# Two stands of four tiled matmul batches per group instead of three stands, in a kernel whose order is a table

## The chip, the cores and the metric

The kernel runs on one core of one Trainium2 chip. The metric is the device time of one execution in microseconds (us), as the median of several runs. Five instruction streams work side by side and meet at semaphores: TensorE (PE in the profile, its weight loads are PEld), VectorE (DVE), ScalarE (ACT), GpSimd (POOL) and SyncE (SP), which issues DMAs here.

## The reference: what is computed

The input x is 128 batches of 128 tokens by 512 features, in float32; adj is a 128 x 128 matrix. Two layers follow each other.

```python
# layer 0: with W1 = W2 = adj, (C - A) is the bias b alone
A = jnp.einsum('od,bdn->bon', adj, x)
pre = A[:, :, None, :] + (C - A)[:, :, :, None]
x = layernorm(x + jnp.max(relu(pre), axis=-1))
# layer 1: 8 heads of 64 features, mask from adj
qkv = x @ w_qkv
attn = softmax(where(adj == 0, -inf, q k^T * 64**-0.5))
o = (attn @ v) @ w_proj + b_proj
x = layernorm(x + o + layernorm(o) * gamma + beta)
```

Because both weights of layer 0 are adj, its branch comes to one number per token: the maximum over the features of adj times x, plus b, clipped at zero.

## The kernel before

Batches are worked in 32 groups of four. Every step of one batch (or of one of a group's twelve dense products) is a small Python function; the table `STEADY` gives each step a place in time relative to its group, `PERIOD` is the distance of two groups, and `group_plan` puts all steps of all groups on one list, which is sorted by place. The steps are then issued in that order, each to its engine. So the places only decide the order in which each engine's queue is filled; at run time an engine takes its queue strictly in that order, and waits where an input or a buffer isn't ready. The first two groups have tables of their own (`FIRST`), and so do the last two (`LAST`); `SETUP` places the weights' preparation. `TWO` says which of the alternating steps go to GpSimd, or into a pair of PSUM banks. `HOMES` names the buffer of each tile, by batch in the group and by group.

The steps, by engine, for batch i of a group (0 to 3; a number behind a step's name is i, or the dense product's number 0 to 11):

- SP: `load` (x, 256 KB), `xrow` and `xcross` (the normalized x is written to DRAM as 16-bit planes and read back by a transposing DMA), `row` and `cross` (the same for the attention weights, 512 KB), `res` (x again, for the residual), `out`.
- PE: `conv` (adj times x, 2 matmuls of 512 columns as float32 needs two passes), `dm` and `dd` (a dense product of q, k or v in three terms: eight matmuls of high and low parts, four of the difference form), `S` (scores, 8 heads), `AV` (attention times v, 8 heads), `po` and `pod` (the output projection, eight and four matmuls).
- DVE: `bn`, `ba`, `cmax` (maximum of conv), `xmask`, `xsub` (high and low part of x), `rest` (adds the difference product), `masked`, `rmax`, `recip`, `wts` (softmax), `omask`, `osub`, `pmain`, `prest`, `n1a`, `n1b`.
- ACT: `norm0`, `xpl`, `main` (evicts the eight-matmul product), `exps`, `pln`, `sq0`, `sq1`, `sq2`, `norm2`, `add0`, and high halves `xhigh`, `ohigh`.
- POOL: `relu`, statistics of a column each (`rstdx`, `shiftx`, `rstd0`, `shift0`, `sm1`, `st1`, `sm2`, `st2`), `resx`, `resb`, `reso` (the residual), and those differences `xd`, `od` and high halves that `TWO` gives it.

The scores use 64 rows of the array (a head has 64 features), and attention times v 64 columns; all other matmuls use 128 by 128. In the steady order S and AV stand next to each other in runs between the other matmuls, called stands here. The products' matmuls are float32r, those of `conv`, `S` and `AV` float32.

Each step's lines are in the functions below: `load` L626, `conv` L630, `S` L863, `AV` L949, the products L817, L818 and L823, `bn` L680, `prest` and `n1b` L1012. Some buffers are few: x tiles (`xt` and `xT`) have four slots, which loads and transposed copies share; the eight PSUM banks are four single ones (`ps1`) and two pairs (`ps2`); `planes` and `xplanes` have one buffer each.

Of the kernel before, what the change touches and what calls it, by code (L numbers as in the profile page):

```python
# [27 lines left out]
PERIOD = 55.65721  # L28
STEADY = {
    'load': [-84.387, -101.525, -92.757, -104.895],  # L30
    'conv': [-75.113, -75.979, -71.238, -73.133],
    'cmax': [-74.046, -74.912, -70.171, -71.594],
    'relu': [-73.282, None, -69.407],
    'bn': [-79.685, -90.339],
    'ba': [-78.963, -87.311],
    'rstdx': [-71.500],
    'shiftx': [-67.749],
    'add0': [None, None, -69.067, -62.343],
    'sq0': [None, None, -68.228, -60.929],
    'rstd0': [None, None, -60.228],  # L40
    'shift0': [None, None, -20.160],
    'norm0': [-66.552, -60.223, -55.338, -56.756],
    'xpl': [-65.714, -57.708, -54.441, -46.941],
    'xrow': [-64.641, -56.635, -53.368, -45.398],
    'xcross': [-61.931, -52.928, -48.082, -41.718],
    'xmask': [-54.951, -43.405, -41.164, -36.407],
    'xsub': [-48.801, -42.437, -37.819, -35.400],
    'xhigh': [-46.997, -35.315, -37.063, -35.835],
    'xd': [-26.327, -29.608, -22.523, -17.793],
    'dm': [4.837, 11.201, 6.655, 16.122, -27.595, -10.169, -22.140, -32.141, -33.960, -23.959, -25.777, -30.323],  # L50
    'dd': [9.383, 10.292, 20.788, 27.152, -12.896, -6.532, -8.350, -5.623, -4.714, -16.490, -7.441, -11.987],
    'main': [7.711, 13.218, 9.668, 20.862, -11.380, -7.877, -11.865, -20.987, -31.942, -21.472, -23.760, -26.046],
    'rest': [10.516, 14.823, 28.292, 38.461, -10.247, -5.049, -3.873, -4.461, -2.608, -11.977, -6.331, -9.059],
    'S': [0.000, 0.997, 13.110, 14.107],
    'masked': [1.644, 5.106, 15.417, 27.161],
    'rmax': [3.380, 8.064, 24.101, 29.327],
    'exps': [4.623, 15.506, 26.003, 35.155],
    'recip': [10.406, 20.865, 29.217, 43.570],
    'wts': [11.110, 22.861, 30.453, 44.268],
    'pln': [13.703, 24.200, 32.382, 51.803],  # L60
    'row': [20.837, 26.467, 34.304, 55.119],
    'cross': [24.197, 29.995, 47.113, 59.806],
    'AV': [37.158, 54.685, 53.762, 70.756],
    'omask': [41.739, 55.758, 58.432, 77.236],
    'osub': [42.962, 56.693, 64.847, 80.884],
    'ohigh': [46.552, 56.528, 63.853, 84.748],
    'od': [47.794, 58.991, 74.103, 86.254],
    'po': [51.853, 58.675, 73.718, 96.599],
    'pod': [57.646, 64.130, 75.536, 100.236],
    'pmain': [60.163, 63.121, 81.492, 101.655],  # L70
    'prest': [61.894, 65.455, 82.210, 102.843],
    'res': [41.103, 53.159, 76.024, 78.628],
    'resx': [52.598, 58.118, 78.904, 82.973],
    'resb': [53.844, 60.258, 80.456, 101.811],
    'reso': [62.664, 71.516, 83.739, 104.286],
    'sq1': [66.881, 66.175, 85.753, 103.922],
    'sm1': [66.639, 71.226, 88.501, 103.613],
    'st1': [68.723, 67.062, 90.348, 105.534],
    'n1a': [69.485, 72.830, 94.712, 105.600],
    'n1b': [77.841, 75.237, 95.973, 108.029],  # L80
    'sq2': [78.635, 93.900, 96.767, 110.927],
    'sm2': [90.058, 96.472, 97.864, 110.751],
    'st2': [94.366, 98.154, 99.952, 125.624],
    'norm2': [95.548, 105.334, 102.729, 130.428],
    'out': [97.230, 106.460, 109.286, 132.611],
# [3 lines left out]
        'load': [-311.682, -309.097, -309.092, -289.177],  # L89
        'conv': [-301.956, -285.978, -284.699, -252.846],  # L90
        'cmax': [-276.686, -268.417, -252.229, -243.444],
        'relu': [-275.480, -258.624, -245.414, -236.373],
        'bn': [-298.400, -272.353, -260.336, -251.012],
        'ba': [-276.256, -271.589, -254.792, -248.969],
        'rstdx': [-272.599, -269.091, -248.273, -238.464],
        'shiftx': [-269.130, -253.340, -240.209, -232.976],
        'norm0': [-266.978, -249.667, -237.355, -228.662],
        'tx': [-266.046, -245.978, -230.203, -224.006],
        'copy': [-248.555, -225.163],
        'pv': [-226.671, -221.380],  # L100
        'keep': [-210.841, -209.446],
        'xmask': [-237.451, -231.282, -228.825, -220.542],
        'xsub': [-232.807, -226.381, -226.376, -184.540],
        'xhigh': [-235.047, -224.785, -216.680, -210.529],
        'xd': [-232.210, -205.597, -206.130, -125.910],
        'dm': [None, None, 8.596, 7.614, -27.333, -7.643, -16.082, -37.145, -46.738, -6.339, -11.225, -36.934],
        'dd': [None, None, 7.519, 13.277, -25.364, -7.365, -10.388, -25.470, -13.330, -4.235, -16.812, -26.914],
        'main': [None, None, 9.424, 14.292, -8.119, -5.070, -13.376, -26.832, -30.312, -2.548, -8.551, -26.673],
        'rest': [None, None, 11.233, 35.409, -6.802, -0.906, -5.599, -18.911, -0.865, 0.048, -7.653, -11.149],
        'S': [0.071, 3.526, 11.673, 10.965],  # L110
        'masked': [4.362, 7.230, 17.266, 20.450],
        'rmax': [4.711, 7.375, 18.562, 27.402],
        'exps': [6.391, 14.172, 25.847, 36.857],
        'recip': [12.522, 19.013, 30.495, 40.437],
        'wts': [13.400, 26.323, 35.020, 43.252],
        'pln': [14.511, 33.217, 37.332, 48.065],
        'row': [24.078, 40.304, 45.297, 48.373],
        'cross': [31.686, 41.648, 45.892, 58.796],
        'AV': [38.517, 48.815, 50.261, 70.407],
        'omask': [43.804, 51.125, 58.512, 81.275],  # L120
        'osub': [44.138, 53.164, 60.683, 86.080],
        'ohigh': [45.476, 55.853, 65.956, 87.153],
        'od': [52.512, 60.084, 71.048, 87.521],
        'po': [48.135, 56.775, 71.054, 93.215],
        'pod': [54.003, 61.222, 76.700, 97.775],
        'pmain': [55.811, 59.410, 82.388, 98.578],
        'prest': [56.183, 64.180, 82.945, 101.590],
        'res': [46.370, 42.491, 71.387, 79.013],
        'resx': [63.966, 47.589, 79.420, 100.786],
        'resb': [70.459, 70.785, 81.534, 105.046],  # L130
        'reso': [70.474, 72.568, 90.218, 105.110],
        'sq1': [63.146, 65.537, 87.020, 104.749],
        'sm1': [69.929, 71.912, 90.063, 105.360],
        'st1': [72.212, 72.233, 94.751, 105.573],
        'n1a': [78.126, 76.071, 96.130, 106.436],
        'n1b': [82.298, 76.869, 96.351, 108.235],
        'sq2': [82.739, 79.519, 97.605, 111.944],
        'sm2': [87.842, 82.457, 97.845, 117.109],
        'st2': [90.386, 87.300, 99.888, 120.030],
        'norm2': [95.187, 93.693, 107.047, 122.559],  # L140
        'out': [99.205, 96.285, 112.844, 132.585],
    },
    {
        'load': [-131.325, -146.629, -109.252, -117.493],
        'conv': [-103.575, -126.260, -90.173, -103.104],
        'cmax': [-94.745, -125.823, -83.341, -89.398],
        'relu': [-80.440, None, -75.846],
        'bn': [-106.480, -139.224],
        'ba': [-99.960, -134.812],
        'rstdx': [-91.047],  # L150
        'shiftx': [-79.188],
        'add0': [None, None, -74.243, -74.248],
        'sq0': [None, None, -69.318, -69.504],
        'rstd0': [None, None, -68.606],
        'shift0': [None, None, 14.252],
        'norm0': [-78.560, -74.678, -62.455, -54.484],
        'xpl': [-77.724, -72.376, -61.942, -52.495],
        'xrow': [-75.147, -66.114, -52.002, -51.491],
        'xcross': [-52.007, -55.219, -51.696, -50.648],
        'xmask': [-51.097, -51.522, -47.743, -46.741],  # L160
        'xsub': [-47.766, -48.031, -45.293, -45.741],
        'xhigh': [-44.210, -49.814, -42.689, -41.925],
# [31 lines left out]
        'n1b': [80.034, 71.944, 89.870, 107.555],  # L194
        'sq2': [83.515, 87.175, 100.626, 112.358],
        'sm2': [85.095, 77.407, 91.265, 112.382],
        'st2': [89.764, 89.887, 102.645, 129.724],
        'norm2': [94.880, 93.286, 102.685, 130.269],
        'out': [99.098, 100.886, 102.826, 130.308],
    },  # L200
# [951 lines left out]
```

## Time and profile before

| | us |
|---|---|
| median of three runs (1845.74 to 1847.9) | 1845.97 |
| the profiled execution | 1842.58 |
| its span | 1840.6 |
| TensorE busy in it | 1804.2 |
| VectorE, ScalarE, GpSimd busy | 1548.9, 1541.5, 1311.4 |
| mean granted TensorE clock | 0.996 |

The span goes from the first to the last instruction. A matmul's row has the time of its start and a modelled duration that overlaps the next one's, so distances of starts are what tells TensorE's pace. A wait is put down to what released it. "x330" behind an engine's busy time is the number of its instructions in the stretch. One line of the DMA view gives how long after its issue a transfer of a tile had landed. A stretch's line has, after the five engines, the granted clock, the DMA engines' share and GB/s.

### The profile page before, as it was taken

The numbers are of one execution on the slowest core, as the hardware profiler recorded it, in microseconds if no ns is written. First come the engines' busy times: TensorE is split into PE (matmuls) and PEld (weight loads), VectorE is DVE, ScalarE is ACT, GpSimd is POOL, SyncE is SP. The second block draws the span as 40 slices with busy tenths as digits, with TensorE's granted clock in tenths as the row PEclk, the third lists the DMA queues.
The fourth block names the chain that finished last, engine by engine and source line by source line (L and its number), as shares of the span: only waits on it lengthen the run. The fifth ranks groups of instructions, "written<-read, shape, count | busy, mean of one in ns | idle before, by whom it ended". The sixth has DMA issues, their size and how long they took to land. (4 is left out here: it accounts for less than half of the span.)

```text
span 1840.6 us, 32730 instructions
## 1 busy us (share of the span) xinstructions
PE 1804.2 (98%) x10541; PEld 1426.1 (77%) x10541; DVE 1548.9 (84%) x2584; ACT 1541.5 (84%) x3927; POOL 1311.4 (71%) x1935
## 2 busy tenths in 40 slices
PE   8999999999999999999999999999999999999995
PEld 5777777778777788777787777787777787777874
DVE  7988888888888888888888888888888888788877
ACT  6988888888888888888888888888888888878865
POOL 4277787677777777777676877776877777667768
PEclk9999999999999999999999999999999999999998
DMA  5556665666575676565676656675656665656641
GB/s 150 173 149 182 170 171 162 163 179 183 150 185 165 158 191 171 157 175 160 175 183 166 170 169 162 174 184 161 180 162 159 185 184 149 178 144 178 155 126 46
DMA packets 486139, 302.91 MB, mean 165 GB/s; under 512 B 399440, under 2 KB 403664, under 8 KB 485968
## 3 DMA queue, kind: packets, MB, share of 16 engines
q1 hardware_dynamic: 485104, 299.70, 60.6%
q8 instruction: 84, 1.38, 0.3%
q10 hardware_dynamic: 864, 1.12, 0.2%
q14 instruction: 87, 0.71, 0.1%
HBM read 72.16 MB, written 131.07 MB: 110 GB/s over the span
## 5 line engine op out<-in xcount | busy, mean ns | idle before, releaser
L902 ACT ACTIVATE e<-e,nmax 128x128 f32<-128x128 f32 x1016 | 393.1, 390 | 34.9 <-DVE nmax L885 34.8
L917 ACT COPY planes<-e 128x2048 uint16<-128x2048 uint16 x124 | 234.9, 1894 | 41.7 <-DMA rows<-planes 20.4
L1018 ACT ACTIVATE square<-o,sum 128x512 bf16<-128x512 f32 x256 | 183.6, 717 | 88.0 <-DVE o L1012 87.0
L1002 POOL TENSOR_SCALAR xb<-xb,sum 128x512 f32<-128x512 f32 x128 | 109.5, 855 | 194.9 <-DMA xb<-in_x_dram 185.7
L1024 POOL TENSOR_TENSOR sum<-sum,mhalf 128x1 f32<-128x1 f32 (+1 forms) x287 | 195.5, 681 | 23.9
L1009 POOL TENSOR_TENSOR xb<-xb,o 128x512 f32<-128x512 f32 x125 | 173.4, 1387 | 35.9 <-DVE o L1012 33.7
L902 ACT ACTIVATION_READ_ACCUMULATOR e<-e,nmax 128x1 f32 x1016 | 191.9, 189 | 0.0
L911 DVE TENSOR_TENSOR e<-e,sums 128x1024 f32<-128x1024 f32 x128 | 175.9, 1375 | 0.1
L1005 POOL TENSOR_TENSOR xb<-xb,beta_sb 128x512 f32<-128x512 f32 x128 | 167.4, 1308 | 4.9
L716 ACT COPY xplanes<-xt 128x1024 uint16<-128x1024 uint16 x124 | 129.1, 1041 | 41.4 <-DMA rowsx<-xplanes 40.5
L1023 POOL TENSOR_SCALAR sum<-sum 128x1 f32<-128x1 f32 (+1 forms) x287 | 122.4, 427 | 56.3 <-ACT square L1018 36.9
L877 DVE SCALAR_TENSOR_TENSOR e<-psc,mask 128x1024 f32<-128x1024 f32 x127 | 154.4, 1216 | 1.3 <-PE psc L863 1.3
L885 DVE TENSOR_REDUCE nmax<-e 128x8 f32<-128x1024 f32 x127 | 151.7, 1195 | 0.1
L643 DVE TENSOR_REDUCE rm<-pa 128x1 f32<-128x512 f32 x128 | 87.7, 688 | 68.0 <-PE pa L632 66.4
L739 DVE TENSOR_SCALAR oxh<-pav 128x512 int32<-128x512 int32 x128 | 87.2, 681 | 64.5 <-PE pav L949 62.8
L949 PEld LDWEIGHTS pav<-eT,v 128*64 128x64 f32 x2048 | 109.8, 137 | 38.1 <-issue 16.4
L863 PEld LDWEIGHTS psc<-qkT 64*128 64x128 f32 x2048 | 119.5, 188 | 18.5 <-issue 17.0
L749 POOL TENSOR_TENSOR x_d<-x_h,x_l 128x512 fp32r<-128x512 f32 x97 | 128.9, 1332 | 6.2 <-DVE x_l L755 6.2
L949 PE MATMUL pav<-eT,v 128*64 128x128 f32 x2048 | 133.2, 277 | 0.0
L863 PE MATMUL psc<-qkT 64*128 64x128 f32 x2048 | 132.3, 279 | 0.6 <-DVE v L846 0.4
L632 PE MATMUL pa<-xt,adjT 128*128 128x512 f32 x256 | 131.1, 615 | 0.5 <-DVE adjT L561 0.4
L1039 DVE SCALAR_TENSOR_TENSOR o<-o,sum,gamma_sb 128x512 f32<-128x512 f32 x128 | 99.4, 778 | 31.0 <-POOL xb L1009 23.8
(4288 smaller groups left out, 5533.3 us busy)
## 6 DMA issues: line engine op xcount, KB each, us to landing
rows<-planes SPq DMA_DIRECT2D x124, 512.0 KB, 3.8
xt<-in_x_dram SPq DMA_DIRECT2D x128, 256.0 KB, 3.6
xb<-in_x_dram SPq DMA_DIRECT2D x128, 256.0 KB, 3.0
out_dram<-o SPq DMA_DIRECT2D x128, 256.0 KB, 3.2
rowsx<-xplanes SPq DMA_DIRECT2D x124, 256.0 KB, 2.8
wraw<-in_L_gnn_w_qkv_dram SPq DMA_DIRECT2D x8, 256.0 KB, 3.6
xT<-rowsx SPq DMA_TRANSPOSE x124, 3.6
eT<-rows SPq DMA_TRANSPOSE x124, 4.4
```

Of the source, the lines that this page charges most:

```text
L632: nc.tensor.matmul(pa[b], adjT, xs[b], start=True, stop=True)
L863: nc.tensor.matmul(psc[:, s, hp, :], qkT[hs, hp, i, :], qkT[hs, KC + hp, i, :], start=not with_mask, stop=not with_mask or hp == HP - 1,)
L877: nc.vector.scalar_tensor_tensor(es[b], pscs.pop(b).rearrange("p s a m -> p (s a) m"), scale, mask_b, op0=ALU.mult, op1=ALU.add,)
L885: nc.vector.tensor_reduce(nmaxs[b], es[b], AX.X, ALU.max, negate=True)
L902: nc.scalar.activation(es[b][:, j, :], src[:, j, :], AF.Exp, bias=nmax[:, j : j + 1], scale=by, accum_out=sums[b][:, j : j + 1],)
L911: nc.vector.tensor_tensor(es[b], es[b], sums.pop(b)[:, :, None].to_broadcast([P, H, P]), op=ALU.mult,)
L917: nc.scalar.copy(pl, es.pop(b).rearrange("p h m -> p (h m)").bitcast(U16).rearrange("p (m s) -> p s m", s=2),)
L949: nc.tensor.matmul(pavs[b][s * HD : (s + 1) * HD, hp, :], v[:, h * HD : (h + 1) * HD], eT[:, s * HP + hp, :], start=True, stop=True,)
L1005: nc.gpsimd.tensor_tensor(xbs[b], xbs[b], beta_sb, op=ALU.add)
L1009: engine.tensor_tensor(xbs[b], xbs[b], os[b], op=ALU.add)
L1018: nc.scalar.activation(square, src, AF.Square, bias=s[:, 0:1], scale=-float(D), accum_out=s[:, 1:2],)
L1024: nc.gpsimd.tensor_tensor(s, s, mhalf[:, :n], op=ALU.pow)
```

## The change

Only tables change: `PERIOD`, the places, `TWO` and `HOMES`. Every step, its operation and its shape stay. TensorE's steady order of one group, before and after (a step with - belongs to the group before, with + to the next, ++ to the one after that; * marks a pair of banks):

```
before  AV2- AV1- S0 S1 pod0- po1- dm0* dm2 pod1- dd0* dd1 dm1 S2 S3 AV3- dm3 po2-* pod2-* dd2
        dm8+ dm7+ dm11+ dd3 dm4+* dm10+ dm9+ dm6+* conv1++ conv0++ AV0 conv3++ dd9+ conv2++ po3-
        dd4+* dd11+ pod3- dm5+ dd6+* dd10+ dd5+ dd7+ dd8+ po0
after   AV1- AV0- S1 S0 dm1 po1-* pod1-* dd1 dm2 dm0 dm3 S2 S3 AV2- AV3- po0-* conv2++ dd0 conv3++
        dd3 conv0++ pod0-* po2- dm4+ dm11+ conv1++ pod2- dm8+ dd2 po3- dm6+* dm9+* dd8+ dd9+* dd4+
        dd11+ dm7+ dm5+ dd6+* dm10+ pod3- dd5+ dd7+ dd10+
```

Before, a group has a stand of four (AV2 AV1 S0 S1), one of three (S2 S3 AV3) and AV0 alone between two `conv`; after, it has two of four. The four `conv`, of which three stood around AV0, each stand alone between products afterwards. `TWO` moves one difference a group from POOL to DVE (five of eight on POOL before, four after) and one high half from POOL to ACT (two of eight before, one after), and pairs other products with double banks. `load` of batch 1 comes right after `xsub` of batch 3 of the group ahead in the shared slot; before, it stood 25 us ahead of its `conv`. The first two and last two groups and the setup have new places too; there the numbers in the new tables span thousands and only sort.

```diff
-PERIOD = 55.65721
+PERIOD = 55.29520
 STEADY = {
-    'load': [-84.387, -101.525, -92.757, -104.895],
-    'conv': [-75.113, -75.979, -71.238, -73.133],
+    'load': [-102.707, -86.431, -98.711, -97.801],
+    'conv': [-89.104, -81.874, -92.654, -90.879],
...
-    'S': [0.000, 0.997, 13.110, 14.107],
+    'S': [0.000, -0.997, 12.113, 13.110],
...
-    'AV': [37.158, 54.685, 53.762, 70.756],
+    'AV': [53.326, 52.403, 69.397, 70.320],
...
 TWO = {
     'bn': [1, 0],
-    'd': [1, 1, 1, 0, 0, 1, 0, 1],
-    'dense': [1, 0, 0, 0, 1, 0, 1, 0, 0, 0, 0, 0],
-    'h': [1, 0, 0, 0, 0, 1, 0, 0],
-    'po': [0, 0, 1, 0],
+    'd': [0, 1, 0, 0, 1, 1, 1, 0],
+    'dense': [0, 0, 0, 0, 0, 0, 1, 0, 0, 1, 0, 0],
+    'h': [0, 1, 0, 0, 0, 0, 0, 0],
+    'po': [1, 1, 0, 0],
...
     'xt': [
-        '01303210321032103210321032103232',
-        '10032103210321032103210321032121',
-        '23210321032103210321032103210300',
-        '32121032103210321032103210321013',
+        '01131313131313131313131313131330',
+        '10222222222222222222222222222213',
+        '23000000000000000000000000000021',
+        '32313131313131313131313131313102',
     ],
...
```

## The prediction

> **What bounds the kernel now.** I read the engines' shares first, then a steady group's stretch, then the matmuls' order and pitch in time, then waits and the end.
>
> ```profile
> PE 1804.2 (98%) x10541; PEld 1426.1 (77%) x10541; DVE 1548.9 (84%) x2584; ACT 1541.5 (84%) x3927; POOL 1311.4 (71%) x1935
> 258.36:313.94 55.58, 55.58 (x330) 44.48 (x329) 46.97 (x80) 47.99 (x123) 40.75 (x61) 1.00 0.64 171
> ```
>
> The second line is one group, from its first score matmul to the next group's: TensorE is never idle and its clock is whole, VectorE idles 8.6 us, ScalarE 7.6, GpSimd 14.8. The busy share alone proves little; the pitch does. Starts of the matmul rows in the timeline:
>
> ```profile
> 538.47 0.39 PE L818 MATMUL pm_('o', 32)_5892<-p_l,ol 128*128 128x512 f32 x1
> 538.79 1.97 PE L949 MATMUL pav<-eT,v 128*64 128x128 f32 x32
> 540.69 2.06 PE L863 MATMUL psc<-qkT 64*128 64x128 f32 x32
> 542.67 1.20 PE L823 MATMUL pd_('o', 32)_5968<-p_d,od 128*128 128x512 f32 x4
> 545.08 0.39 PE L817 MATMUL pm_('o', 33)_5980<-p_h,oh 128*128 128x512 f32 x1
> ...
> 553.47 0.39 PE L818 MATMUL pm_(9, 1)_6075<-w_l,x_l 128*128 128x512 f32 x1
> 553.79 2.06 PE L863 MATMUL psc<-qkT 64*128 64x128 f32 x32
> 555.77 1.09 PE L949 MATMUL pav<-eT,v 128*64 128x128 f32 x16
> 558.75 0.39 PE L817 MATMUL pp_('o', 34)_6156<-p_h,oh 128*128 128x512 f32 x1
> ...
> 575.75 0.39 PE L818 MATMUL pp_(10, 6)_6322<-x_l,w_l 128*128 128x512 f32 x1
> 575.98 1.88 PE L632 MATMUL pa<-xt,adjT 128*128 128x512 f32 x4
> 577.78 1.09 PE L949 MATMUL pav<-eT,v 128*64 128x128 f32 x16
> 578.81 1.12 PE L632 MATMUL pa<-xt,adjT 128*128 128x512 f32 x2
> 579.37 1.50 PE L823 MATMUL pd_(10, 9)_6374<-x_d,w_d 128*128 128x512 f32 x4
> 580.70 1.02 PE L632 MATMUL pa<-xt,adjT 128*128 128x512 f32 x2
> 583.40 0.84 PE L823 MATMUL pp_(10, 4)_6274<-x_d,w_d 128*128 128x512 f32 x3
> ```
>
> Product matmuls (L817, L818, L823) start every 0.2267 us; a group has 192. Call a run of AV (L949) and S (L863) between others a stand. What one costs is how late the next products come. Four: after 538.47 the next product was due at 538.70, the one ten further at 540.97; it starts at 545.08, so 4.11. Three: due 553.70 + 8 x 0.2267 = 555.51, started 558.75: 3.24. The lone AV with four conv: due 575.98 + 12 x 0.2267 = 578.70, started 583.40: 4.70. Sum: 192 x 0.2267 + 4.11 + 3.24 + 4.70 = 55.58, the whole group. So nothing but the order of TensorE's own work sets a steady group; 55.58 separates the first scores of most neighbouring groups.
>
> A weighing. By the Trainium skill ("Trainium Kernel Development and Optimization", Performance Expectations) matmul busy time is a bad measure, and the share of weight loads a good one. At 77% of weight loads that would leave a quarter of TensorE free and make the PE-order term below 0; the sum would be 1842. The row above, in which pitch times count fills the group, decides against it.
>
> Outside the steady part: the first scores start at 48.49 us; TensorE ends at 1828.5 of 1840.6. One group is far off: 60.39 us between the first scores of groups 28 and 29. Its cause, from the waits between 1595 and 1613 us:
>
> ```profile
> DVE bnst L680 <- DMA xt<-in_x_dram: 3.4, 1, 3.4
> PE pd_('o', 109)_17866 L823 <- DVE o L1012: 2.5, 1, 2.5
> ```
>
> bn of batch 120 stands first in VectorE's queue while its load is in flight; prest 108 is behind it, and pod 109 needs prest's bank. The clock then falls (0.91 granted over 1600 to 1620).
>
> **The change, part by part.** The profiled execution took 1842.58 us (span 1840.6, 2.0 around it), 3.4 below the median of 1845.97; I sum against 1842.58 and add 3.4.
>
> *Stands.* Per group before: AV2 AV1 S0 S1; S2 S3 AV3; AV0 between conv0 and conv3. After: AV1 AV0 S1 S0; S2 S3 AV2 AV3; four conv, each alone between products. A stand of four costs 4.11 whichever batches are in it (two AV, two S, one change between them). A lone conv: without conv2 at 580.70 the product after po3's eight would start at 580.70 + 8 x 0.2267 = 582.51; it starts at 583.40: 0.89. After: 4.11 + 4.11 + 4 x 0.89 = 11.78 against 12.05: 0.27 less, 55.31 a group. Over the whole order the stands fall from 99 to 69, thirty at 0.27: **-8.1**. Bounds: -6.9 if each lone conv costs 0.01 more than conv2 showed (30 groups, four conv), -9.3 if 0.01 less.
>
> *Load of batch 120.* In SP's queue it now stands ahead of xcross 116, two DMA_TRANSPOSEs earlier. bn 120 now stands between rest 5 and rest 10 of group 28. Between load and bn the order itself lays: row110 and xrow116 put the load 0.7 us behind xpl116; then two norms (0.8 each) and main7 (0.58) on ScalarE, whose bank pod3 takes; then pod3, dd5, dd7 (0.91 each), rest 7 and rest 5 (0.6 each by spacing): 6.1 - 0.7 = 5.4 us at least, against a load's landing of
>
> ```profile
> DMA to landing us min/median/max: 2.5/3.6/6.3
> ```
>
> so the 4.81 us over 55.58 should go but for 0.4, as the groups beside it have: **-4.4**, bounds -4.8 and -3.5 (landing at 6.3: rest 10 is 0.9 late and S113's last quarter waits).
>
> *Helpers moved.* POOL loses one difference a group (1.30) and one high half (1.5 to 1.6), VectorE gains a difference (0.68), ScalarE a high half (0.62). VectorE becomes 47.7 and ScalarE 48.6 of 55.3. What hides them is TensorE's own 55.3; were it gone, ScalarE would cost 0.62 a group. **0**, bounds 0 and +3 for queueing (a tenth of a microsecond in each of 30 groups).
>
> *Added exposure.* Two feeds of TensorE have less cover. (a) S1 now starts behind dd10, AV1, AV0; the last quarter of S1 needs rest 10. Cover 1.9 us (two AV) plus 0.7, need 0.7 of rest: 1.9 left, where VectorE isn't behind. (b) load1 of the group after next waits until xsub3 has freed the only slot of batches 1 and 3, and conv1 needs it; before, load1 was issued 25 us ahead of conv1. VectorE's queue from masked0 through xsub3 adds to 20.5 us by the rows' spacing, from S0's end 2.1 us into the group: free at 22.6, or 22.9 by way of dd3, rest3, xsub3. TensorE reaches conv1 at 28.8 (products and stands as costed). 5.9 us for issue and landing: 2.3 spare at the median 3.6, minus 0.4 at the longest, less VectorE's idle in between. Behind load1 SP holds row0, and behind that the crosses. (c) Banks change: pod3 now takes main7's; cover dm5, dd6, dm10, 4.5 us, for ScalarE's four norms and copies ahead of main7. I take 0.05 us a group, the value of a stall in one group of ten: **+1.5**, bounds 0 and 1.3 x 29 = +38 (every load at the longest landing with 0.9 of VectorE idle).
>
> *Both ends.* Same operations, new order. Head: TensorE is idle 0.38 + 0.41 + 0.44 + 1.28 + 0.31 = 2.8 us before the first scores; walking wmask, wsub, wl by their 0.42, 0.69, 0.63 in the new order I find dm8 at the same 24 us, dm4 0.5 late, the first scores at 48 to 49. **0**, bounds -3 (that idle goes) and +5 (two parts of weights each late by a chain of 2.4). Tail: idle before the last product is 1.11 + 2.01 + 0.40 + 2.40 + 2.11 = 8.0, and 12.1 behind it. The last scores (S127) now have AV123 behind them too, so the last batch starts its softmax one AV (0.9) earlier against TensorE's end: **-1**, bounds -8 and +8 (that idle gone, or as much again).
>
> ```profile
> 1810.00:1829.00 19.00, 11.71 (x59) 8.14 (x57) 15.28 (x29) 7.57 (x16) 17.57 (x27) 1.00 0.08 29
> 1829.00:1841.00 12.00, 0.00 (x0) 0.00 (x0) 4.43 (x10) 4.66 (x9) 6.77 (x15) 0.50 0.18 66
> ```
>
> These show the tail held by VectorE and POOL, each near full up to 1829, and then by chains.
>
> Sum: -8.1 - 4.4 + 0 + 1.5 + 0 - 1 = -12.0: profiled 1830.6, median 1834.0.
>
> **Rivals.** (1) *The ends or joins give back.* A load in front of bn cost 4.8 once; one such join in the new order, or a tail worse by 8.0, leaves -12.0 + 4.8 to 8.0: 1839 to 1842, say 1840. For it: nothing shows the new tail. Against: the bounds go both ways. (2) *Slower: load1 becomes a wait in every group.* conv1 waits for the landing; TensorE, and all behind it, shifts by that much. It cancels the gain from 13.5 / 29 = 0.47 us a group; at 0.75 a group it costs 21.8 on -13.5: +8, 1854. For it: loads of up to 6.3, and SP's order puts row0's 512 KB right behind. Against: 2.3 spare at the median. (3) *The steady saving doesn't appear*, because a conv alone costs more than conv2 showed (0.07 more on each of four) or bank waits eat it: -4.4 - 1 + 1.5: 1842; with a new join stall 1847, say 1845.
>
> **How the numbers follow.** Forecast 70%, its own range 1827 to 1840 (tail and head bounds halved, as both ends at their limits together are rare). Rival 1: 14%, all faster. Rival 2: 8%, above 1850. Rival 3: 8%, mostly within 0.2%. A measurement here tells 0.2%, 3.7 us: faster is below 1842.3. Faster 0.70 + 0.13 = 0.83; same 0.01 + 0.07 = 0.08; slower 0.08 + 0.01 = 0.09. Leaving out rival 2 and the outermost tenth of the others, the range is 1826 to 1845.
>
> **What would show it.** Right: neighbouring groups' first scores 55.3 us apart; S and AV rows of 32 and 32 matmuls in two stands, none of 16; lone conv followed by products 0.89 late; no long wait of bnst for xt near group 28; the end still 12 us behind the last product. Wrong: a PE wait of pa on xt in each group (rival 2); groups of 55.6 with waits of TensorE on ScalarE or VectorE (rival 3); first scores later than 52 us, or over 14 us behind the last product (rival 1).

## The result and the profile after

The changed kernel takes 1852.59 us (median of 16 runs) where the kernel before took 1847.24 beside it: a ratio of 1.0033, 95% interval 1.0022 to 1.0044. It is slower by 0.33%; the forecast was 1834.0 us with a range up to 1845. The profiled execution took 1856.64 us, its span is 1854.9. That is 4 us above its median, and the profiled execution of the kernel before (1842.58) is 4.7 us below 1847.24: the two profiles differ by 14.1 us, the medians by 5.35. Sizes read from these two profiles are therefore larger than in a usual pair of executions; what causes them is tested below by ratios of medians. Line numbers of the changed kernel are two higher than before (AV is L951, S L865, the products L819, L820 and L825, conv L634).

The engines' shares of the kernel after, and two of its steady groups (first scores to first scores of the next group) and its end. A line of the second kind has the stretch, its length, busy time of PE, PEld, DVE, ACT and POOL with their counts, granted clock, DMA share and GB/s:

```profile
PE 1809.0 (98%) x10541; PEld 1425.9 (77%) x10541; DVE 1627.0 (88%) x2614; ACT 1552.6 (84%) x3959; POOL 1277.6 (69%) x1873
```

```profile
823.91:880.51 56.60, 55.92 (x331) 44.38 (x329) 50.00 (x81) 48.20 (x124) 40.30 (x59) 1.00 0.62 168
880.51:936.39 55.88, 55.88 (x331) 44.42 (x329) 50.04 (x81) 48.21 (x124) 40.09 (x59) 1.00 0.66 170
1820.80:1839.60 18.80, 15.14 (x64) 10.64 (x64) 13.68 (x22) 9.33 (x18) 14.82 (x26) 0.91 0.15 57
1839.60:1854.90 15.30, 0.00 (x0) 0.00 (x0) 6.73 (x15) 6.40 (x13) 10.12 (x22) 0.61 0.14 52
```

A steady group should be 55.31 us long. These two are 56.60 and 55.88, at a full clock. TensorE's busy time is no help in finding the rest: in the second group it fills the whole 55.88 us, since the rows' lengths are modelled; only distances of starts show it. Laid out by the first scores of the groups, the two profiled spans (1840.6 and 1854.9) differ so:

| stretch | before | after | after minus before |
|---|---|---|---|
| start to first scores of group 3 | 205.6 | 204.4 | -1.2 |
| groups 3 to 27, 25 distances, mean | 55.749 | 56.357 | +15.2 |
| groups 28, 29, 30 | 171.6 | 169.4 | -2.2 |
| first scores of group 31 to the end | 69.7 | 72.2 | +2.5 |

So the ends moved little and the loss is in the steady groups, where a gain of 0.27 us a group was forecast. What TensorE waits for, and what stands behind it, from the waits of the kernel after (total us, times, longest):

```profile
ACT xplanes L718 <- DMA rowsx<-xplanes: 101.8, 52, 4.3
PEld pa L634 <- DVE ol L969: 19.0, 26, 1.2
DVE o L1041 <- POOL sum L1029: 13.7, 17, 0.9
PE pa L634 <- DVE ol L969: 8.5, 16, 0.8
```

conv (L634) waits for osub (L969): conv3 takes the PSUM bank of AV2's result, and VectorE's osub2 frees it. VectorE's n1a (L1041) waits for a column sum on GpSimd (L1029, `sm1`), and ScalarE waits two and a half times as long in all as before (101.8 us against 40.5) for the one `xplanes` buffer. The same wait in the kernel before:

```profile
ACT xplanes L716 <- DMA rowsx<-xplanes: 40.5, 28, 2.9
```

To see where the microsecond goes, I take the distance from each step's first matmul to the next step's, mean over groups 3 to 27, minus the least that such a transition shows in any kernel of this study (0.906 us behind the four matmuls of a `dd`, 1.813 behind the eight of a `dm`, 1.333 from dd0 to conv3, 0.455 behind a conv):

| transitions of the kernel after | over the least, us a group |
|---|---|
| dd0 to conv3 0.437, conv3 to dd3 0.137 | 0.57 |
| dd8 to dd9 0.157, dd9 to dd4 0.131, the next two 0.014 | 0.30 |
| dm2 to dm0 0.110, dm0 to dm3 0.038 | 0.15 |
| what is left up to the mean | 0.03 |

Together 1.05 over 55.31, which is 56.36. The least values are those forecast: four operations in a stand and a conv alone cost what the kernel before showed.

The second row in one group: dd9 was due 4 x 0.2267 us behind dd8, at 865.49. It writes the second half of a pair of banks whose first half main9 on ScalarE reads until 865.62, and it starts at 865.66. In the third row dm0 waits for the bank that main1 reads (one of its longest waits, in group 5):

```profile
864.58 1.07 PE L825 MATMUL pd_(15, 8)_9448<-x_d,w_d 128*128 128x512 f32 x4
865.03 0.59 ACT L844 ACTIVATE qkT<-pp_(15, 9)_9429 128x512 f32<-128x512 f32 x1
865.66 1.20 PE L825 MATMUL pp_(15, 9)_9429<-x_d,w_d 128*128 128x512 f32 x4
PEld pm_(5, 0)_3518 L819 <- ACT v L844: 1.0, 1, 1.0
```

### The profile page after: what moved, and what is told of

It reads as the page before. It is cut to its first block, busy times and chain, and to the rows that moved or that the text cites. A ratio compares the mean times of both kernels' runs of the same rounds, so it can differ in the third digit from the quotient of the medians.

```text
span 1854.9 us, 32975 instructions
## 1 busy us (share of the span) xinstructions
PE 1809.0 (98%) x10541; PEld 1425.9 (77%) x10541; DVE 1627.0 (88%) x2614; ACT 1552.6 (84%) x3959; POOL 1277.6 (69%) x1873
## 4 chain that ended last, share of the span: by engine, by line
PE 70%; DVE 9%; ACT 6%; POOL 6%; DMA 5%; issue 3%; SPq 0%; DVEq 0%; ACTq 0%; POOLq 0%
PE pa L634 5%; DMA rowsx<-xplanes 4%; PE psc L865 3%; PE pav L951 3%; DVE o L1014 2%; ACT xplanes L718 1%; DVE qkT L848 1%; POOL sum L1026 1%; ACT square L1020 1%; DVE oxh L741 1%; ACT oh L747 1%; POOL od L751 1%; POOL sum L1025 1%; DVE ol L969 1%; DVE o L1041 1%
## 5 line engine op out<-in xcount | busy, mean ns | idle before, releaser
L718 ACT COPY xplanes<-xt 128x1024 uint16<-128x1024 uint16 x124 | 129.2, 1042 | 102.7 <-DMA rowsx<-xplanes 101.8
L1007 POOL TENSOR_TENSOR xb<-xb,beta_sb 128x512 f32<-128x512 f32 x128 | 176.9, 1383 | 5.0
L751 POOL TENSOR_TENSOR od<-oh,ol 128x512 fp32r<-128x512 f32 x93 | 122.8, 1320 | 61.2 <-DVE ol L969 21.2
L913 DVE TENSOR_TENSOR e<-e,sums 128x1024 f32<-128x1024 f32 x128 | 158.8, 1240 | 1.1
L634 PE MATMUL pa<-xt,adjT 128*128 128x512 f32 x256 | 136.1, 617 | 11.0 <-DVE ol L969 8.5
L1029 POOL TENSOR_SCALAR sum<-sum 128x1 f32<-128x1 f32 x256 | 108.2, 428 | 48.7 <-DVE o L1014 44.5
L1025 POOL TENSOR_SCALAR sum<-sum 128x1 f32<-128x1 f32 (+1 forms) x287 | 89.7, 313 | 72.9 <-ACT square L1020 52.5
L865 PEld LDWEIGHTS psc<-qkT 64*128 64x128 f32 x2048 | 119.6, 188 | 18.6 <-issue 16.8
L865 PE MATMUL psc<-qkT 64*128 64x128 f32 x2048 | 132.5, 279 | 0.2 <-DVE qkT L848 0.2
L747 ACT ACTIVATE oh<-oxh 128x512 fp32r<-128x512 f32 x124 | 77.4, 624 | 61.2 <-DVE oxh L741 54.6
L951 PE MATMUL pav<-eT,v 128*64 128x128 f32 x2048 | 126.8, 276 | 1.3 <-ACT eT L942 1.3
L745 POOL TENSOR_SCALAR x_h<-xm 128x512 fp32r<-128x512 f32 x32 | 62.1, 1942 | 92.4 <-DVE xm L741 92.2
L951 PEld LDWEIGHTS pav<-eT,v 128*64 128x64 f32 x2048 | 110.4, 137 | 17.5 <-DVE qkT L848 9.9
```

The costliest lines, as they stand in the source:

```text
L634: nc.tensor.matmul(pa[b], adjT, xs[b], start=True, stop=True)
L865: nc.tensor.matmul(psc[:, s, hp, :], qkT[hs, hp, i, :], qkT[hs, KC + hp, i, :], start=not with_mask, stop=not with_mask or hp == HP - 1,)
L913: nc.vector.tensor_tensor(es[b], es[b], sums.pop(b)[:, :, None].to_broadcast([P, H, P]), op=ALU.mult,)
L951: nc.tensor.matmul(pavs[b][s * HD : (s + 1) * HD, hp, :], v[:, h * HD : (h + 1) * HD], eT[:, s * HP + hp, :], start=True, stop=True,)
L1007: nc.gpsimd.tensor_tensor(xbs[b], xbs[b], beta_sb, op=ALU.add)
```

## The experiments

All start from the changed kernel and change the steady table, in groups 2 to 29, unless said. Ratios are to the kernel before on the same chip, whose median differs from chip to chip (1842.7 to 1847.2), so ratios are compared, not times; the times expected for e1 to e11 were reckoned from 1852.6 and 1837.4, measured beside 1847, that of e12 from e10's 1835.5 beside 1842.7. "Conv3", "dense" and "dm" below are the three rows of the table above in us a group, measured in the same way (e4's dense row with the wait of dd8 itself).

| run | ratio (95%) | mean group | conv3 | dense | dm |
|---|---|---|---|---|---|
| changed kernel | 1.0033 (1.0022 to 1.0044) | 56.36 | 0.57 | 0.30 | 0.15 |
| e1_dd9_later | 1.0047 (1.0034 to 1.0060) | 56.52 | 0.42 | 0.74 | 0.05 |
| e2_xpl_later | 0.9975 (0.9965 to 0.9985) | 55.85 | 0.25 | 0.29 | 0.00 |
| e3_osub_sm | 0.9949 (0.9937 to 0.9962) | 55.80 | 0.02 | 0.28 | 0.15 |
| e4_xd_gpsimd | 1.0202 (1.0188 to 1.0216) | 57.30 | 0.38 | 1.59 | 0.06 |
| e5_dd_by_bank | 1.0065 (1.0050 to 1.0080) | 56.45 | 0.27 | 0.89 | 0.01 |
| e6_osub_alone | 1.0030 (1.0018 to 1.0042) | 56.29 | 0.59 | 0.29 | 0.09 |
| e7_all | 1.0037 (1.0024 to 1.0050) | 56.19 | 0.00 | 0.87 | 0.00 |
| e8_all_tail | 1.0041 (1.0029 to 1.0053) | 56.19 | 0.00 | 0.87 | 0.00 |
| e9_xpl_osub_sm | 0.9965 (0.9951 to 0.9978) | 55.62 | 0.00 | 0.27 | 0.00 |
| e10_and_dm9 | 0.9958 (0.9946 to 0.9971) | 55.61 | 0.02 | 0.00 | 0.00 |
| e11_sm_alone | 0.9959 (0.9947 to 0.9972) | 55.74 | 0.01 | 0.29 | 0.11 |
| e12_main7 | 0.9929 (0.9916 to 0.9943) | 55.45 | 0.09 | 0.00 | 0.00 |

**One suspected wait each.**

e1, dd9 behind dd4:

```diff
-    'dd': [18.802, 5.658, 32.310, 20.577, -14.802, -5.711, -9.347, -4.801, -16.621, -15.712, -3.892, -13.893],
+    'dd': [18.802, 5.658, 32.310, 20.577, -15.712, -5.711, -9.347, -4.801, -16.621, -14.802, -3.892, -13.893],
```

> The changed kernel with one swap in the steady order: the second half of dense 9 (dd9) goes behind dd4 instead of ahead of it. Theory A (three separate chains make the excess of about 1.07 us a group over 55.30): dd9 stands right behind main9 in the order, both touch one pair tile, and the row dd8 to dd9 plus dd9 to dd4 is 0.30 us a group over the pitch; with 0.9 us more cover it goes, 28 groups x 0.30 = 8.4 us: 1852.6 -> about 1844, ratio to the kernel before 0.998, and dd8 to the next product 0.91 us. Rival B (VectorE, 88% busy, is the bound and TensorE only waits in another place): 1850 or more, and conv3's wait grows by what dd9's loses.

No gain: the wait moved, as rival B said, but for another reason than VectorE. dd9 itself came free, and dd4 in its place waited for main4, which reads dd4's bank and follows main9 directly. Two lines of TensorE and two of ScalarE in one group (start, length, last the idle time and its releaser):

```profile
859.96 1.07 PE L825 MATMUL pd_(15, 8)_9448<-x_d,w_d 128*128 128x512 f32 x4
860.37 0.59 ACT L844 ACTIVATE qkT<-pp_(15, 9)_9429 128x512 f32<-128x512 f32 x1
860.85 0.59 ACT L844 ACTIVATE qkT<-pm_(15, 4)_9298 128x512 f32<-128x512 f32 x1
861.49 1.20 PE L825 MATMUL pd_(15, 4)_9458<-x_d,w_d 128*128 128x512 f32 x4 [0.47 <-ACT qkT L844]
```

ScalarE's eviction of dense 4 ends at 861.44, and dd4 starts at 861.49. As the dense row grew by 0.44, conv3's and dm's shrank by 0.25: a TensorE held up in one place gives the others time to catch up, so the three rows do not add up as if each stood alone.

e2, xpl3 behind ohigh0 on ScalarE:

```diff
-    'xpl': [-65.018, -61.071, -55.172, -51.614],
+    'xpl': [-65.018, -61.071, -55.172, -47.700],
```

> The changed kernel with the plane copy of the third batch (xpl3) moved on ScalarE behind main1, sq1 of batch 1 and ohigh0, so that its wait for the landing of the row before (xrow2) holds none of them. Theory A: main1 starts 2.7 us earlier, the waits of dm0 and dm3 for its bank go (0.165 us a group, 4.6 us), ohigh0, od0, sm1 and n1a1 come about 1.2 us earlier, and of conv3's wait for osub2 (0.56 us a group) about half goes, 8 us: about 1840, between 1836 and 1848. If ScalarE's lateness does not reach VectorE: 1848, the bank waits alone. Rival B (VectorE is the bound by its own length): 1848 or more, osub2 as late as before.

As theory A: the dm row is gone and conv3's more than halved. Two waits of this kernel:

```profile
ACT xplanes L718 <- DMA rowsx<-xplanes: 20.4, 26, 4.0
PEld pa L634 <- DVE ol L969: 10.9, 26, 1.3
```

e3, osub0 ahead of pmain1 on VectorE and sm1 of batch 1 ahead of od0 on GpSimd:

```diff
-    'osub': [61.762, 54.898, 73.583, 83.496],
+    'osub': [60.200, 54.898, 73.583, 83.496],
-    'sm1': [94.925, 66.819, 97.846, 109.930],
+    'sm1': [94.925, 63.270, 97.846, 109.930],
```

> The changed kernel with osub0 ahead of pmain1 on VectorE (it fills the wait of pmain1 for the other half of its pair tile) and sm1 of batch 1 ahead of od0 on GpSimd. Theory A: VectorE's two jumps of lateness (0.85 us at pmain1, 0.87 us at n1a1) shrink by 0.69 and up to 0.87 us, osub2 comes 1.3 us earlier, and conv3's wait goes: 0.4 to 0.56 us a group, 11 to 16 us: 1837 to 1842. Rival B: osub2 no earlier than 0.7 us, 1847 or more.

As theory A; conv3's row falls from 0.57 to 0.02. e6 and e11 below take its two halves apart.

e4, one difference back on GpSimd (this entry of `TWO` holds in all groups but the first):

```diff
-    'd': [0, 1, 0, 0, 1, 1, 1, 0],
+    'd': [0, 1, 1, 0, 1, 1, 1, 0],
```

> The changed kernel with the difference of the third batch (xd2) given back to GpSimd, as the kernel before has it. VectorE loses 28 instructions of 1.78 us, GpSimd gains as many of 1.3 us. Theory A: xd2 lies behind the late stretch and VectorE has idle time there, so nothing on TensorE's path moves: 1849 to 1856; or a little slower, if xd1 and xd2 in a row on GpSimd make dd8 wait. Rival B (VectorE is the bound by its busy time): 50 us of VectorE's work less, a good part of the 1.07 us a group goes: 1840 or less.

Both missed the size. VectorE has 31 differences of x less (62 that took 58.4 us, where 93 took 103.4), and the kernel is 1.7% slower than the changed one. In the new order dd8 comes so early that GpSimd cannot deliver both differences in time; dd8 waits in nearly every group:

```profile
PEld pd_(14, 8)_8826 L825 <- POOL x_d L751: 1.7, 1, 1.7
PEld pd_(12, 8)_7582 L825 <- POOL x_d L751: 1.7, 1, 1.7
```

At these places in the queues, the new order needs this helper on VectorE. The new wait is longer than anything a freer VectorE could have gained, so e4 alone does not settle rival B. e3 and e12 do: conv3's row is 0.02 and 0.09 there, and VectorE is busy for 1633.6 and 1633.7 us, more than the 1627.0 of the changed kernel.

**Another order of the four products, half of e3, and a sum.**

e5, dd8, dd11, dd9, dd4:

```diff
-    'dd': [18.802, 5.658, 32.310, 20.577, -14.802, -5.711, -9.347, -4.801, -16.621, -15.712, -3.892, -13.893],
+    'dd': [18.802, 5.658, 32.310, 20.577, -13.893, -5.711, -9.347, -4.801, -16.621, -14.802, -3.892, -15.712],
```

> The changed kernel with the steady order dd8, dd11, dd9, dd4 in place of dd8, dd9, dd4, dd11. In e1 the wait only moved: dd4 takes the bank that main4 reads, and main4 comes right behind main9, so dd4 waited 0.6 us in dd9's place. dd11's bank was freed long before (by pmain3), so it can go first and give main9 and main4 each 0.9 us or more. Theory A (the waits of dd8 to dd4 are a chain of their own, 0.28 us a group): 28 x 0.28 = 7.8 us less, 1852.6 -> about 1845, every one of these four rows at 0.91 us. Rival B (TensorE is paced by VectorE and the time comes back at conv3): 1850 or more, conv3's wait grows by 0.2 us or more.

A miss, and by a wrong reading of mine: dd11's bank had not been free for long. pmain3 on VectorE frees it, and it ends 0.06 us before dd11 starts, 0.7 us late:

```profile
862.19 1.07 PE L825 MATMUL pd_(15, 8)_9448<-x_d,w_d 128*128 128x512 f32 x4
863.10 0.68 DVE L988 SCALAR_TENSOR_TENSOR o<-pm_('o', 55)_9385,bias_sb 128x512 f32<-128x512 f32 x1
863.84 1.20 PE L825 MATMUL pd_(15, 11)_9458<-x_d,w_d 128*128 128x512 f32 x4 [0.58 <-DVE o L988]
```

dd9, dd4 and dd11 each have a releaser that ends just before their turn in the changed order, so an exchange among them loses.

e6, the osub half of e3 alone:

```diff
-    'osub': [61.762, 54.898, 73.583, 83.496],
+    'osub': [60.200, 54.898, 73.583, 83.496],
```

> The changed kernel with only the first half of e3: osub0 ahead of pmain1 on VectorE; sm1 of batch 1 stays behind od0 on GpSimd. If the lateness of osub2 is the sum of two jumps (0.85 us at pmain1, 0.87 us at n1a1, where the second waits for sm1): n1a1 still waits for sm1, so most of what osub0 gains is lost there again, and conv3's wait (0.60 us a group with its follower) shrinks by a third or less: 1847 to 1853. If pmain1's wait is the only cause: as e3, 1837 to 1840.

As the first case: conv3's row stays at 0.59. pmain1's wait for the other half of its pair of banks, which holds VectorE 1.6 us in each group, is not by itself what makes osub2 late. Here it shrinks to some 0.8 us, in front of osub0, and VectorE loses the gain again where n1a waits for sm1 (13.7 us in all in the changed kernel):

```profile
DVE o L1041 <- POOL sum L1029: 25.0, 28, 1.2
```

e7, e2 with e3 and e5 (the diff is theirs, put together: `xpl` -47.700, `osub` 60.200, `sm1` 63.270 and e5's `dd`):

> The changed kernel with e2, e3 and e5 together. Theory A (three chains, each its own): from e3's steady mean of 55.80 us a group, e2 takes the waits of dm0 and dm3 (0.15) and e5 those of dd8 to dd4 (0.28): 55.37, against 55.31 that the stands alone give; from e3's 1837.4 that is 0.43 x 28 = 12 us less: 1825, between 1822 and 1829, and a ratio to the kernel before of 0.988. Rival B: something else stops TensorE next, above 1832. Rival C (the stands of four do not save 0.27 us a group): the mean stays at 55.6 or more, 1831 or more.

The total missed because of e5's wrong order, but the rest is telling: all rows but the dense one stand at their least.

e8, e7 and in the last group od of batch 126 on VectorE:

```diff
                     two = TWO["first_" + which] if first and k == 0 else TWO[which][k : k + G]
+                    if last and kind == "od":
+                        two = [1, 1, 0, 0]
```

> e7 with one operation more moved: in the last group alone the difference of batch 126 (od) goes from GpSimd to VectorE. In the changed kernel pod126 waits 2 to 3 us for it behind two instructions on batch 127's residual, and GpSimd carries the end (15.3 us from the last product to the end, 12.1 in the kernel before). If the wait sets the end: 2 to 3 us less than e7. If GpSimd's own list of work sets it: its 1.25 us less. If VectorE, which then carries it, sets it: no gain.

No gain, the third case: from the first scores of group 31 to the end it took 72.8 us, 72.1 in e7. pod126 now waits 3.4 us for VectorE in place of 2.0 for GpSimd. The end of the changed kernel is not explained by this one operation.

**Down to the least of every row.**

e9, e2 with e3:

```diff
-    'xpl': [-65.018, -61.071, -55.172, -51.614],
+    'xpl': [-65.018, -61.071, -55.172, -47.700],
-    'osub': [61.762, 54.898, 73.583, 83.496],
+    'osub': [60.200, 54.898, 73.583, 83.496],
-    'sm1': [94.925, 66.819, 97.846, 109.930],
+    'sm1': [94.925, 63.270, 97.846, 109.930],
```

> The changed kernel with e2 and e3 together, the dense order as in the changed kernel. In e7 every row of the steady order stood at its least except dd8 to the next (0.72 us over) and the one behind the wait (0.13); with the order dd8, dd9, dd4, dd11 that pair of rows costs 0.26 to 0.30 us over. Theory A: 56.19 - 0.85 + 0.28 = 55.62 us a group, 0.18 less than e3, 28 x 0.18 = 5 us: 1832, between 1829 and 1836. Rival B (waits trade places): as e3 or above, 1837 or more.

The group's mean is the expected 55.62, but the time is a miss: at 0.9965 it is no faster than e3's 0.9949, as rival B had it. The two intervals overlap, so 0.18 us a group more or less than e3 isn't told apart here.

e10, e9 with dense 9 ahead of dense 6 (places of dm and main, and the two pairs' banks in the steady groups):

```diff
-    'dm': [8.385, 0.992, 6.567, 10.204, -30.215, -11.166, -20.258, -12.984, -24.803, -18.439, -8.438, -28.397],
+    'dm': [8.385, 0.992, 6.567, 10.204, -30.215, -11.166, -18.439, -12.984, -24.803, -20.258, -8.438, -28.397],
-    'main': [11.413, 4.633, 15.224, 17.123, -15.937, -6.862, -16.962, -7.347, -21.241, -16.422, -6.377, -25.821],
+    'main': [11.413, 4.633, 15.224, 17.123, -15.937, -6.862, -16.422, -7.347, -21.241, -16.962, -6.377, -25.821],
     'pp': [
-        '10001010101010101010101010101010',
+        '10110101010101010101010101010110',
...
-        '01110101010101010101010101010101',
+        '01001010101010101010101010101001',
```

> e9, and dense 9 goes first: dm9 and dm6 change places on TensorE, main9 and main6 on ScalarE, and the two pairs their banks, in the steady groups. main9 then ends 0.5 us earlier and is off the start of dd9; no other bank comes free later. Theory A: every row at its least, 55.33 us a group, e9 less 28 x 0.28 = 8 us: 1824, between 1821 and 1829, ratio to the kernel before about 0.989. Rival B (as in e1 and e5, the wait goes to the next bank): 1830 or more. Rival C (the stands of four do not save): 55.6 a group, 1831 or more.

Rival B: the dense row is at its least, and 0.27 us came up at pod3, which takes the bank that main7 reads (dm10 to pod3 0.13, pod3 to dd5 0.13, the next two 0.01). In one group main7 ends at 808.34, and pod3, due one pitch behind dm10's last matmul (808.06), at 808.29, starts at 808.40:

```profile
807.77 0.57 ACT L844 ACTIVATE qkT<-pm_(14, 7)_8868 128x512 f32<-128x512 f32 x1
808.40 1.20 PE L825 MATMUL pd_('o', 51)_8927<-p_d,od 128*128 128x512 f32 x4
```

The prediction had named this feed, with 4.5 us of cover; the cover is spent on a run of ScalarE that has no idle time, and TensorE now came 0.3 us earlier. Most groups are then 55.57 us long, 0.01 from those before the change, and yet held by another engine.

e11, the sm1 half of e3 alone, one instruction of 0.23 us moved ahead of three steps in GpSimd's queue:

```diff
-    'sm1': [94.925, 66.819, 97.846, 109.930],
+    'sm1': [94.925, 63.270, 97.846, 109.930],
```

> The changed kernel with only the second half of e3: sm1 of batch 1 ahead of od0 on GpSimd, osub0 behind prest1 as in the changed kernel. If n1a1's wait for sm1 is what makes osub2 late: most of e3's 15 us, 1838 to 1842. If both jumps of lateness are needed to be taken away: 1844 to 1850, and e3 is more than the sum of e6 and this.

The first case, at the expected size (1838 to 1842 beside 1847 is 0.995 to 0.997): ratio 0.9959 where the changed kernel has 1.0033, the whole loss gone, and 0.41% gained of the 0.65% that was forecast. The chain can be read in one group of both kernels. After the change (lines of ScalarE, GpSimd, VectorE and TensorE in order of time; the group's first scores are at 767.01):

```profile
775.16 1.05 ACT L718 COPY xplanes<-xt 128x1024 uint16<-128x1024 uint16 x1 [3.93 <-DMA rowsx<-xplanes]
777.31 0.62 ACT L747 ACTIVATE oh<-oxh 128x512 fp32r<-128x512 f32 x1
778.01 1.29 POOL L751 TENSOR_TENSOR od<-oh,ol 128x512 fp32r<-128x512 f32 x1 [1.27 <-ACT oh L747]
...
782.25 0.23 POOL L1029 TENSOR_SCALAR sum<-sum 128x1 f32<-128x1 f32 x1
782.51 0.77 DVE L1041 SCALAR_TENSOR_TENSOR o<-o,sum,gamma_sb 128x512 f32<-128x512 f32 x1 [0.92 <-POOL sum L1029]
...
788.19 0.69 DVE L969 TENSOR_TENSOR ol<-pav,oxh 128x512 fp32r<-128x512 f32 x1
788.93 1.13 PE L634 MATMUL pa<-xt,adjT 128*128 128x512 f32 x2 [0.51 <-DVE ol L969]
```

The same group in e11, first scores at 757.41:

```profile
765.58 1.05 ACT L718 COPY xplanes<-xt 128x1024 uint16<-128x1024 uint16 x1 [3.85 <-DMA rowsx<-xplanes]
767.09 0.23 POOL L1029 TENSOR_SCALAR sum<-sum 128x1 f32<-128x1 f32 x1
...
768.43 1.29 POOL L751 TENSOR_TENSOR od<-oh,ol 128x512 fp32r<-128x512 f32 x1 [1.12 <-ACT oh L747]
...
771.92 0.74 DVE L1041 SCALAR_TENSOR_TENSOR o<-o,sum,gamma_sb 128x512 f32<-128x512 f32 x1
...
777.57 0.69 DVE L969 TENSOR_TENSOR ol<-pav,oxh 128x512 fp32r<-128x512 f32 x1
778.65 1.02 PE L634 MATMUL pa<-xt,adjT 128*128 128x512 f32 x2
```

Counted from the first scores, sm1 runs at 15.24 us after the change and at 9.68 in e11, n1a at 15.50 and 14.51, osub2 at 21.18 and 20.16, conv3 at 21.92 and 21.24. ScalarE waits as long in both (3.93 and 3.85). The input of sm1 was there all along (prest1 on VectorE had ended by 775.29, 7 us before sm1 ran); it stood behind od0, whose input was not, and behind two column steps. Three of e11's waits, to set beside those of the changed kernel:

```profile
ACT xplanes L718 <- DMA rowsx<-xplanes: 98.2, 52, 4.1
PEld pa L634 <- DVE ol L969: 1.5, 2, 1.3
DVE o L1041 <- POOL sum L1029: 0.9, 2, 0.5
```

e12, e10 with main7 ahead of two norms on ScalarE:

```diff
-    'main': [11.413, 4.633, 15.224, 17.123, -15.937, -6.862, -16.422, -7.347, -21.241, -16.962, -6.377, -25.821],
+    'main': [11.413, 4.633, 15.224, 17.123, -15.937, -6.862, -16.422, -8.900, -21.241, -16.962, -6.377, -25.821],
```

> e10, and main7 ahead of two norms of the next batches on ScalarE (norm02 and norm01). In e10 the rows dd8 to dd4 came to their least, but dm10 to pod3 and pod3 to dd5 grew by 0.13 us each: pod3 takes main7's bank, and main7 ends 0.3 us before it is due, at the end of a run of ScalarE without idle. Theory A: with main7 1.5 us earlier all rows stand at their least, 55.33 us a group, 28 x 0.26 = 7 us less than e10's 1835.5: 1828, ratio to the kernel before 0.992. Rival B (ScalarE's run, not one bank, holds TensorE: the wait goes to dd5, whose bank main5 frees next): 55.55 or more, 1834 or more.

Close to theory A, with the lowest ratio of the study: 0.9929, where 0.992 was expected. The rows of dd8 to dd4 and of pod3 are at their least. Of its 24 distances from group 4 to group 28, 19 lie between 55.30 and 55.39 us; one of them:

```profile
700.77:756.11 55.34, 55.34 (x331) 44.56 (x329) 50.40 (x81) 48.09 (x124) 40.22 (x59) 1.00 0.64 172
```

The 0.12 us of the mean over 55.33 are single groups, in most of which conv3 waits again (0.09 a group).

## Why the prediction was wrong

**Stands, -8.1: right in mechanism and size, but not to be had alone.** 55.31 us a group was forecast, and most of e12's groups are 55.31 to 55.35 long. Its ratio, 0.9929, is close to the forecast's 1834.0 / 1845.97 = 0.9935, in part by luck: join and tail, below, did not come as forecast, and in its profile the start up to group 3 is 4.9 us shorter, where 0 was forecast. In the changed kernel the same saving is there, row by row, under 1.05 us of waits.

**Added exposure, +1.5: the step that failed.** It measured 1.05 us a group, 26 us over groups 3 to 27 of the profiled execution. The step listed three feeds: S1 on rest10, conv1 on load1 and pod3 on main7. The first never held TensorE: S1's rows stand at their least in all steady groups; of the second the waits show a single one, 0.7 us long; the third costs 0.015 us a group until e10 takes the earlier waits away. The three waits that mattered were not on the list: conv3's bank freed by osub2, dd9 right behind main9 on one pair of banks, and dm0 and dm3 behind a late main1. The upper bound of +38 held the size, but it was written for load1, and the value of 1.5 was taken for feeds that I had looked at, with nothing for those I had not.

**What lay behind it: "helpers moved, 0".** The engines' own busy time was treated as the question (GpSimd idle 14.8 us a group, ScalarE 7.6, VectorE 8.6), and it was not: e3 and e12, with VectorE as busy as in the changed kernel, show that its additional work is not what costs, and e11 shows that 0.23 us of GpSimd in the wrong place of its queue cost 0.62 us a group by the two profiles (some 0.5, as an estimate, by the ratios: 0.74% of 1847 over 28 groups). One difference moved "from POOL to DVE" is also only the net count of `TWO`: xd0, xd2 and od3 went to VectorE, and od0 and od2 to GpSimd. The prediction priced the net and did not see od0 arrive in GpSimd's queue. The chain is: landing of xrow2, xpl3 (one buffer), ohigh0 on ScalarE, od0 on GpSimd, sm1 behind it, n1a on VectorE, osub2 behind it, conv3. e2 breaks it at its second link, e11 at its fifth, and they take back 0.58 and 0.74 of the 0.98% between forecast and result; that is shown. Moved steps change what stands ahead of whom in every queue. The prediction walked SP's queue past the moved load, VectorE's from masked0 to xsub3 and ScalarE's ahead of main7; it walked none back from osub2, main1 or main9.

**Load of batch 120, -4.4: the wait went, the time did not.** No bnst line for xt is left in the kernel after. But groups 28 and 29 are 59.53 us apart, not 55.6; before, 60.39. So 0.9 us came of the 4.4. In place of that wait stand, among others (waits between 1613 and 1673 us):

```profile
PE pa L634 <- ACT qkT L844: 1.4, 1, 1.4
PE pm_(28, 0)_17830 L819 <- ACT v L844: 0.7, 1, 0.7
PE pp_(29, 9)_18134 L825 <- ACT qkT L844: 0.5, 1, 0.5
PE pp_('o', 108)_17919 L819 <- DVE e L879: 0.3, 1, 0.3
```

The steady waits are not the reason: e12, clean in the steady part, has 59.69 there, and all kernels with the new order have 57.9 to 59.7. The groups behind this join have tables of their own, but no experiment worked on it, so the cause stays open.

**Ends.** The head was within its bounds: the first scores of all came at 49.80 us, where 48 to 49 was forecast and 48.49 measured before, and those of group 3 came 1.2 us earlier than before. The tail was taken at -1 and measured +2.5, within -8 to +8: 15.3 us behind the last product where 12.1 was, and no experiment here says why.

**The rivals.** Rival 3 (bank waits eat the saving) is what happened, and its sign, waits of TensorE on ScalarE or VectorE in each group, is the one that was seen; but it had 8% and a price of 1845. That price let the steady saving of 0.27 us a group vanish; the waits took 1.05. Rival 1 happened in part: the join gave 3.5 us less than forecast, the tail is 3.5 worse than forecast, and its sign of more than 14 us behind the last product was seen. Rival 2, load1, did not happen.

## What to carry to other kernels

When the order of queues changes, list every buffer that the bound engine takes and who frees it, and then walk the freeing engine's queue backwards, past small instructions too: a cheap step whose input is ready is as late as the waiting step ahead of it. Idle time of an engine says nothing about that. And when several short waits stand on one engine, an experiment on one of them can mislead: e2 and e11 each took one away and gained, but in e1, e5 and e10 the wait that was removed came back at the next bank.

## What the runs showed of the hardware

The difference of x costs VectorE more than the 0.68 us at which I priced it. In the kernel after, 93 of them took 1.135 us on average, those of the third batch 1.78, and all of VectorE's differences together went from 66.2 to 124.7 us, 58 more, where 31 more of them at 0.68 make 21. Beside each long one stands a two-input instruction of GpSimd that is long as well, 1.81 us where it takes 1.29 elsewhere. VectorE and GpSimd in one group:

```profile
861.52 2.35 DVE L751 TENSOR_TENSOR x_d<-x_h,x_l 128x512 fp32r<-128x512 f32 x2
861.51 1.81 POOL L1011 TENSOR_TENSOR xb<-xb,o 128x512 f32<-128x512 f32 x1 [0.93 <-DVE o L1014]
```

The first of the two differences takes 0.65 us, GpSimd's addition is longer by 0.52, and the second difference ends some 0.55 us behind the addition, which is what taking turns would give: 0.6, then 1.3, then 0.6. The Trainium skill ("SBUF — State Buffer", SBUF: two separate sides) states that a VectorE operation with two SBUF inputs and a GpSimd operation that reads SBUF hold a shared pair of ports for the whole instruction, and the other one is blocked. These rows agree with it. So does e4, where the second difference is gone: in its steady groups the addition still takes 1.81 us beside the first, which takes 0.65. No run here took the addition away. The long differences are not what held TensorE: in e12 the same 93 take 102.9 us, and most of its groups stand at 55.31 to 55.35.
